# Order of a graph layer's first stage: a reload behind the last load, edge placing behind the statistics, first edge groups sooner

## The chip, the cores and the metric

The kernel runs on one core of a Trainium2 chip. The metric is the device time of one execution in microseconds (us). The engines are named as in the profile: PE (TensorE matmul), PEld (its weight loads), DVE (VectorE), ACT (ScalarE), POOL (GpSimd) and SP (SyncE, which here only issues DMAs). Each engine works through its own queue in order.

## The reference

One layer of a graph network on 10000 nodes with 512 features and 160000 edges, sorted by destination; everything is float32.

```python
xn = layernorm(x)
h  = xn @ W                                           # graph part
agg = segment_sum(h[src] * edge_weight[:, None], dst)
gnn = relu(agg + bias)
q, k, v = split(xn @ w_qkv.T)                         # 8 heads of 64
q = softmax(q, over a head's features) * 64 ** -0.5
k = softmax(k, over the nodes)
ctx = k.T @ v                                         # per head
mix = layernorm((q @ ctx) @ w_out.T) * gamma
x = x + gnn + mix
x = x + ffn(layernorm(x))                             # experts, weighted by a router on the mean row
```

## The kernel before

The nodes lie in 20 chunks: 19 of 128 partitions with 4 rows each (SUB = 4) and a last one of 68 partitions. The work has three stages, which the trace shows at 0 to 161 us, 161 to some 1850 us (the edges run through all of it) and from there to the end (the experts' products).

**Start.** `normal_rows` loads a chunk (L416, on SP's queue), takes its statistics on DVE (L166, L167), finishes them on POOL (L169, L171, L419, L420), normalises on ACT (L422) and stores the rows to a scratch tensor `xn_d` in DRAM (L424, ACT's queue). A pool of seven tiles (`a_io`) holds the chunks in flight. Meanwhile chunks 0 and 1 (`EARLY = 2`, the two that `KEPT` keeps in memory) do their keys and queries by plain matmuls (L209), exp and softmax (L885, `softmax_rows` with L192 to L194, `kacc` at L844), and the context sum over nodes `pc` (L911), which DVE copies or adds into `G` (L918, L914). Transposes on PE are L201, their evictions L203.

**Edge lists.** Four lists of 625 KB (`src_sb`, `w_sb`, `dst_sb`, `row_sb`; L446 to L451) are loaded on SP's queue after the statistics of `LISTS = 10` chunks. The generator `place_edges` (L454 to L518) then works out on DVE where in its window of nodes each edge falls; it is taken on by two steps after each further chunk (L428), and what is left of it at chunk 2 (L858).

**From chunk 2 on** keys and queries come from seven products instead of eight (`seven`, L246, with matmuls at L243); DVE makes the sums that they need: of the weights (`kq_sum`, L233 to L236, once) and of the rows (`xs_b`, L226 to L229, for each chunk). The rows come back from `xn_d` (`rows_of`, L834). Between products `work(us)` is called, which counts time in units of the code (`PRODUCT = 0.83` for a product of 128 by 128 by 512) and puts edge groups into PE's order as they come due: the number of tiles due is `done[1] / PACE` with `PACE = 0.9`. At chunk 2 the counter starts at

```python
done[1] = -16 * PACE
```

so nothing comes due for the first 16 tiles' worth of units.

**An edge group** has 8 tiles of 128 edges (4 from the 97th group on; 1250 tiles in all). For a tile, POOL gathers 128 rows of `xn_d` by index (`msg`, L583; 24 buffers in pool `edge_m`), DVE builds the selection matrix (`sel`, L589 and L591), PE multiplies (`pm`, L601), ACT copies the sum out (L604) and stores it to `part_d` (L605). Sums of nodes that cross windows are carried on by DMAs on POOL's queue (L673).

**Stage two** starts at about 1100 us. It mixes the queries with the context matrix and gathers the edge sums by row on POOL (`at`, L1017), while edge groups go on at `ROW_PACE = 0.96`; the last group is summed at about 1850 us. Then the experts' products follow, which don't touch the edges.

PE's order is the order of the code (`manual_schedule`, L708). The other engines' orders are set by the scheduler from readiness; `behind(inst, other)` (L157) makes it put one instruction after another, as an order only and without a semaphore. A buffer that lies over an older tile's memory also waits for the last user of that tile: `edge_m` is opened after `norm_ctx.close()` (L860), over the memory of the loads and of the placing's scratch tiles.

Of the kernel before, what the change touches and what calls it, by code (L numbers as in the profile page):

```python
# [12 lines left out]
ALU = mybir.AluOpType  # L13
# [7 lines left out]
SUB = 4  # L21
EPS = 1e-5
HEAD = 64
# [4 lines left out]
FAR = 1.0e5  # L28
EARLY = 2
ROWS_IN = 1.6  # L30
LISTS = 10
CHECKED = 5
KEPT = 2
PRODUCT = 0.83
PACE = 0.9
# [21 lines left out]
def gps_layer_kernel(  # L57
# [19 lines left out]
    nc = tc.nc  # L77
    N, D = x.shape
# [11 lines left out]
    chunks = []  # L90
# [8 lines left out]
    def tokens(t, c):  # L99
        b, r = chunks[c]  # L100
        return t[b : b + r * SUB, :].rearrange("(p s) d -> p s d", s=SUB)
# [38 lines left out]
    xn_d = dram.tile([N, D], F32, name="xn_d")  # L140
# [16 lines left out]
    def behind(inst, other):  # L157

        tc.add_manual_dep(inst.ins, other.ins.name, mybir.DependencyInfo(
            mybir.DependencyClass.NoSync, mybir.DependencyReason.SCHED_ONLY), reason="order of work")  # L160
# [27 lines left out]
    def softmax_rows(q, r, s):  # L188

        q3 = q[:r, s, :].rearrange("p (h e) -> p h e", e=HEAD)  # L190
        qs = small.tile([P, D // HEAD], F32, name="qs")
        nc.vector.tensor_reduce(qs[:r], q3, axis=AX.X, op=ALU.add)  # L192
        nc.vector.reciprocal(qs[:r], qs[:r])
        nc.vector.tensor_tensor(q3, q3, qs[:r, :, None].to_broadcast([r, D // HEAD, HEAD]), ALU.mult)  # L194

    def transposed(o, t, r, psum, tag, by_act=(1, 3)):

# [190 lines left out]
    with ExitStack() as ph:  # L388
# [16 lines left out]


        normal = []
        placing = []
        last_stats = [None]

        def normal_rows(n):

            for c in range(len(normal), min(len(normal) + n, NCH)):
                r = chunks[c][1]
                xt = (xp if c < KEPT else a_io).tile([P, SUB, D], F32, name="xn")
                nc.sync.dma_start(xt[:r], tokens(x, c))  # L416
                mv = small.tile([P, SUB, 2], F32, name="mv")
                last_stats[0] = row_stats(xt, r, mv, on_pool=True)
                nc.gpsimd.tensor_tensor(mv[:r, :, 0], mv[:r, :, 0], mv[:r, :, 1], ALU.mult)  # L419
                nc.gpsimd.tensor_scalar(mv[:r, :, 0], mv[:r, :, 0], -1.0, None, op0=ALU.mult)  # L420
                for i in range(SUB):
                    nc.scalar.activation(xt[:r, i, :], xt[:r, i, :], AF.Identity,  # L422
                                         bias=mv[:r, i, 0:1], scale=mv[:r, i, 1:2])
                nc.scalar.dma_start(tokens(xn_d, c), xt[:r])  # L424
                normal.append(xt)
                if len(normal) == LISTS:
                    placing.append(place_edges(*edges_listed()))
                for _ in range(2 if placing else 0):  # L428
                    next(placing[0], None)

        zero = tmp.tile([P, D], F32, name="zero")
        nc.vector.memset(zero, 0.0)
# [4 lines left out]
        place = ep.tile([P, NET], F32, name="place")  # L437
# [16 lines left out]
        def place_edges(dst_sb, row_sb):  # L454


            nc.vector.tensor_scalar(row_sb, row_sb, 2, None, op0=ALU.arith_shift_right)
            yield
            nc.vector.memset(bases[:, 0:1], 0.0)
            nc.vector.memset(bases[:, NW:], FAR)  # L460
            nc.vector.tensor_copy(bases[:, 1:PAIRED],
                                  row_sb[:, 2 : 2 * PAIRED].rearrange("p (w j) -> p w j", j=2)[:, :, 0])
            nc.vector.tensor_copy(bases[:, PAIRED:NW], row_sb[:, 2 * PAIRED :])
            yield
            gap = tmp.tile([P, NW], F32, name="gap")
            nc.vector.tensor_tensor(gap, bases[:, 1:], bases[:, :NW], ALU.subtract)
            yield
            nc.vector.tensor_copy(place, dst_sb)
            yield

            def by_window_of(t, per_window, o, op):

                nc.vector.tensor_tensor(
                    o[:, : 2 * PAIRED].rearrange("p (w j) -> p w j", j=2),
                    t[:, : 2 * PAIRED].rearrange("p (w j) -> p w j", j=2),
                    per_window[:, :PAIRED, None].to_broadcast([P, PAIRED, 2]), op)
                nc.vector.tensor_tensor(o[:, 2 * PAIRED :], t[:, 2 * PAIRED :], per_window[:, PAIRED:NW], op)

            nodes = tmp.tile([P, NW], F32, name="nodes")
            nc.vector.tensor_scalar(nodes, bases[:, :NW], float(SUB), None, op0=ALU.mult)  # L480
            yield
            by_window_of(place, nodes, place, ALU.subtract)
            yield

            nc.vector.memset(jump[:, 0:1], 1.0)
            nc.vector.tensor_scalar(jump[:, 1:], gap[:, : NW - 1], -1.0, float(WIN // SUB), op0=ALU.mult, op1=ALU.add)
            yield

            beyond = tmp.tile([P, NET], F32, name="beyond", tag="whole")
            good = tmp.tile([P, NET], F32, name="good", tag="row")  # L490
            nc.vector.tensor_scalar(nodes, gap, float(SUB), None, op0=ALU.mult)
            yield
            by_window_of(place, nodes, beyond, ALU.is_ge)
            yield
            nc.vector.tensor_scalar(nodes, nodes, float(SUB), None, op0=ALU.add)
            yield
            by_window_of(beyond, nodes, good, ALU.mult)
            yield
            nc.vector.scalar_tensor_tensor(place, place, float(SUB), good, op0=ALU.add, op1=ALU.subtract)
            yield  # L500
            nc.vector.scalar_tensor_tensor(good, place, float(SUB), beyond, op0=ALU.is_lt, op1=ALU.is_equal)
            yield
            nc.vector.scalar_tensor_tensor(good, place, float(WIN), good, op0=ALU.is_lt, op1=ALU.mult,
                                           accum_out=count[:, 0:1])
            yield
            nc.vector.tensor_scalar(good[:, :NW], gap, 0.0, None, op0=ALU.is_ge)
            yield
            nc.vector.scalar_tensor_tensor(good[:, : NW - 1], gap[:, : NW - 1], float(WIN // SUB), good[:, : NW - 1],
                                           op0=ALU.is_lt, op1=ALU.mult, accum_out=count[:, 1:2])
            yield  # L510
            nc.vector.tensor_scalar(good[:, CHAINED:NW], gap[:, CHAINED:], 0.0, None, op0=ALU.is_gt)
            nc.vector.tensor_reduce(count[:, 2:3], good[:, CHAINED:NW], axis=AX.X, op=ALU.add)
            yield

            for i, (n, w) in enumerate(AT_HAND):
                nc.vector.tensor_scalar(count[:, 3 + i : 4 + i], bases[:, w : w + 1],
                                        float((chunks[n][0] if n < NCH else N) // SUB), None, op0=ALU.is_ge)
            spans_hold()  # L518
# [164 lines left out]
        done = [0, 0.0]  # L683
# [146 lines left out]
        def rows_of(c):  # L830
            if c < KEPT:
                return normal[c]
            xn = xp.tile([P, SUB, D], F32, name="xn")
            nc.sync.dma_start(xn[: chunks[c][1]], tokens(xn_d, c))  # L834
            return xn

        def turned_rows(c, xn):
# [4 lines left out]
        def finish(o, ek, r, at):  # L842
            if o is ek:
                nc.vector.tensor_tensor(kacc[:r], kacc[:r], ek[:r, at, :], ALU.add)  # L844
            else:
                softmax_rows(o, r, at)

        wk = kvp.tile([P, KB, D], F32, name="wk")
        nc.sync.dma_start(wk, w_qkv_t[:, D : 2 * D].rearrange("(k p) d -> p k d", p=P))
# [4 lines left out]
        xn = rows_of(0)  # L854
        xnT = turned_rows(0, xn)
        for c, (_, r) in enumerate(chunks):
            if c == EARLY:
                for _ in placing[0]:  # L858
                    pass
                norm_ctx.close()  # L860
                pools["w"] = edge_ctx.enter_context(tc.tile_pool(name="edge_w", bufs=3))
                done[1] = -16 * PACE
                pools["m"] = edge_ctx.enter_context(tc.tile_pool(name="edge_m", bufs=24,
                                                                 reuse_waits="tile"))
            if c + 1 < EARLY:
# [5 lines left out]
            if c < EARLY:  # L871
                for o, w in ((ek, wk), (qt, wq)):
                    sums = []
                    for s in range(SUB):
# [8 lines left out]
                        for i, po in enumerate(sums):  # L883
                            at = s + 1 - len(sums) + i
# [17 lines left out]
                        finish(qt, ek, r, q)  # L902
            if c + 1 == EARLY:
                normal_rows(NCH)
                xn_next = rows_of(c + 1)
            if c + 1 < NCH:
                xnT = turned_rows(c + 1, xn_next)
# [26 lines left out]
            if c + 1 < NCH:  # L934
                xn = xn_next
# [127 lines left out]
        for c, (_, r) in enumerate(chunks):  # L1063
            ot, at = mixed.pop(0), ats.pop(0)
# [30 lines left out]
            if c == NCH - 1:  # L1095
# [3 lines left out]
                                           op0=ALU.mult, op1=ALU.mult)  # L1099
            if c < NCH - 1:  # L1100
                for s in range(SUB):
                    nc.vector.scalar_tensor_tensor(xsum[:r], ot[:r, s, :], mv[:r, s, 1:2], xsum[:r],
                                                   op0=ALU.mult, op1=ALU.add)
# [5 lines left out]
            if c == NCH - 2:  # L1109
# [7 lines left out]
                xn = rows_in(0)  # L1117
# [252 lines left out]
    with tc.manual_schedule(engines={mybir.EngineType.PE}):  # L1370
# [13 lines left out]
        xt = residual_rows(0)  # L1384
        for c in range(NCH):
            if c + 1 < NCH:
                xn = rows_in(c + 1)
# [6 lines left out]
            xt = nxt  # L1394

    any_more = nc.values_load(n_more[0:1, 0:1], min_val=0, max_val=1)
    with tc.If(any_more > 0):
# [9 lines left out]
        for c, (_, r) in enumerate(chunks):  # L1407
            n = SUB * r
            xn = rows_in(c)
# [3 lines left out]
            xt = fp.tile([P, SUB, D], F32, name="xt", bufs=2)  # L1413
            nc.sync.dma_start(xt[:r], z_d[c])
            hT = []
            for f in blocks:
                m, at = fsz[f], (f - NBASE) * P
# [55 lines left out]
```

## Time and profile before

| | us |
|---|---|
| median of 5 runs | 3304.11 |
| lowest and highest | 3296.22, 3306.65 |
| the profiled execution | 3305.32 |
| its span | 3303.6 |
| PE busy | 3194.3 (97%) |
| DVE busy | 1771.6 (54%) |
| POOL busy | 1314.9 (40%) |
| ACT busy | 833.9 (25%) |
| mean busy share of the DMA engines, first 100 us | 0.97 |
| clock granted to PE, mean | 0.987 |

The rows of a timeline give the start in us, the length in us, the engine, the line of the code, the operation, the output and inputs by the program's names, and the number of instructions taken together; in square brackets stands how long the engine had been idle and what ended the wait. A row of waits names the engine, the tile and line that waited, what it waited for, the total in us, the number of times and the longest. SPq and ACTq are DMA issues on the queues of SP and ACT. In fp32 each matmul of the code shows as two rows' worth of instructions (x4 is two matmuls of the code).

### The profile page before, as it was taken

Reading aid. Unit: us, or ns where it says so; the run is one execution under the profiler, and the core shown is the slowest. Engines: PE = TensorE matmul, PEld = TensorE weight load, DVE = VectorE, ACT = ScalarE, POOL = GpSimd, SP = SyncE. Lnnn points to the kernel's source line nnn. Section 1 sums busy time; section 2 is a strip of 40 time slices with the busy share of each in tenths; the row PEclk is TensorE's granted clock in tenths of the full one; section 3 lists DMA queues with packets and bytes.
Section 4 is the critical chain, followed back from the end, with each engine's and each line's share of the span. In section 5 each row is a group of like instructions: output and inputs, shape, how many; then the busy total and the mean of one; then the engine's idle time right before and its main releaser. Section 6 shows DMA issues by size and latency. Waiting matters only on the chain. (4 is left out here: it accounts for less than half of the span.)

```text
span 3303.6 us, 36142 instructions
## 1 busy us (share of the span) xinstructions
PE 3194.3 (97%) x12819; PEld 1899.0 (57%) x12819; DVE 1771.6 (54%) x3902; ACT 833.9 (25%) x1674; POOL 1314.9 (40%) x1421
## 2 busy tenths in 40 slices
PE   5899999999999999999998979999999999999998
PEld 3344444444443433333333358888888888888886
DVE  6655555555555356566665565445544554445533
ACT  5422222222222122222222142222232222222211
POOL 3377777777776777777777300000000000000000
PEclk8899999999999999999999989999999999999999
DMA  9678889888888999999999822121212212121111
GB/s 386 243 241 282 264 275 315 261 281 256 282 267 239 346 340 353 337 352 345 361 334 306 240 65 64 51 90 52 62 54 64 77 51 64 51 90 51 53 38 40
DMA packets 216735, 654.39 MB, mean 198 GB/s; under 512 B 34425, under 2 KB 74361, under 8 KB 188831
## 3 DMA queue, kind: packets, MB, share of 16 engines
q0 software_dynamic: 104096, 354.29, 33.3%
q1 hardware_dynamic: 69992, 175.33, 16.1%
q10 hardware_dynamic: 42452, 122.31, 9.5%
q8 instruction: 105, 1.72, 0.2%
q14 instruction: 90, 0.74, 0.1%
HBM read 491.21 MB, written 166.63 MB: 199 GB/s over the span
## 5 line engine op out<-in xcount | busy, mean ns | idle before, releaser
L583 POOL DMA_INDIRECT msg<-xn_d,src_sb x1250 | 1234.2, 987 | 431.6 <-issue 210.2
L601 PE MATMUL pm<-msg,sel 128*32 128x512 f32 x2504 | 363.9, 603 | 19.9 <-DMA msg<-xn_d,src_sb 17.5
L209 PE MATMUL pg<-wq,aT 128*128 128x512 f32 (+1 forms) x640 | 291.1, 602 | 0.0
L209 PE MATMUL po<-G,qT 128*128 128x512 f32 (+1 forms) x640 | 290.2, 600 | 0.0
L911 PE MATMUL pc<-xn,ek 128*128 128x512 f32 (+1 forms) x640 | 286.1, 597 | 0.0
L604 ACT COPY part<-pm 128x512 f32<-128x512 f32 x217 | 126.9, 585 | 626.9 <-PE pm L601 581.5
L601 PEld LDWEIGHTS pm<-msg,sel 128*32 128x32 f32 x2504 | 67.5, 109 | 283.1 <-issue 191.0
L209 PEld LDWEIGHTS pg<-wq,aT 128*128 128x128 f32 (+1 forms) x640 | 115.0, 187 | 175.6 <-issue 160.8
L243 PE MATMUL px<-xnT,w_sb 128*128 128x256 f32 (+1 forms) x800 | 204.9, 379 | 7.0 <-DVE u L1290 7.0
L209 PEld LDWEIGHTS po<-G,qT 128*128 128x128 f32 (+1 forms) x640 | 114.9, 187 | 162.9 <-issue 158.2
L166 DVE BATCH_NORM_STATS2 st<-ot 128x6 f32<-128x512 f32 (+1 forms) x160 | 110.5, 691 | 179.7 <-ACT ot L1052 179.0
L243 PE MATMUL p<-kq_sum,xs_b 128*128 128x512 f32 (+1 forms) x432 | 200.7, 600 | 0.0
L911 PEld LDWEIGHTS pc<-xn,ek 128*128 128x128 f32 (+1 forms) x640 | 118.3, 191 | 139.6 <-issue 131.5
L243 PE MATMUL px<-w_sb,hh 128*128 128x256 f32 (+1 forms) x800 | 185.8, 379 | 0.0
L243 PE MATMUL py<-xs,w_sum 128*128 128x256 f32 (+1 forms) x800 | 185.7, 375 | 0.0
L243 PE MATMUL py<-w_sum,hh 128*128 128x256 f32 (+1 forms) x800 | 179.2, 379 | 0.0
L243 PEld LDWEIGHTS px<-xnT,w_sb 128*128 128x128 f32 x800 | 150.7, 192 | 30.2 <-DVE u L1290 10.4
L243 PEld LDWEIGHTS px<-w_sb,hh 128*128 128x128 f32 (+1 forms) x800 | 150.3, 188 | 22.8
L243 PEld LDWEIGHTS py<-w_sum,hh 128*128 128x128 f32 (+1 forms) x800 | 150.0, 188 | 22.7
L243 PEld LDWEIGHTS py<-xs,w_sum 128*128 128x128 f32 x800 | 150.2, 191 | 20.1
L243 PEld LDWEIGHTS p<-kq_sum,xs_b 128*128 128x128 f32 (+1 forms) x432 | 78.0, 187 | 116.1 <-issue 89.8
L351 ACT ACTIVATE xn<-xn,st_all 128x128 f32<-128x128 f32 x288 | 114.8, 481 | 99.8 <-DMA xn<-x_d 94.1
(298 smaller groups left out, 4570.4 us busy)
## 6 DMA issues: line engine op xcount, KB each, us to landing
part_d<-part ACTq DMA_DIRECT2D x217, 256.0 KB
msg<-xn_d,src_sb POOLq DMA_INDIRECT x1250
xn<-in_x SPq DMA_DIRECT2D x19, 1024.0 KB
xn_d<-xn ACTq DMA_DIRECT2D x19, 1024.0 KB
qT_d<-qT ACTq DMA_DIRECT2D x19, 1024.0 KB
qT<-qT_d SPq DMA_DIRECT2D x19, 1024.0 KB
xt<-in_x SPq DMA_DIRECT2D x19, 1024.0 KB
x_d<-ot SPq DMA_DIRECT2D x19, 1024.0 KB
```

The source lines that it names most:

```text
L166: nc.vector.bn_stats(st[:r, s, :], t[:r, s, :])
L209: nc.tensor.matmul(po[:r, :], t[:, kb, s * r : (s + 1) * r], w[:, kb, :], start=kb == 0, stop=kb == KB - 1)
L243: nc.tensor.matmul(o, lhs[j], rhs[j], start=start and j == 0, stop=stop and j == n - 1, skip_group_check=True)
L351: nc.scalar.activation(xn[:, s, b * P : (b + 1) * P], xn[:, s, b * P : (b + 1) * P], AF.Identity, bias=st[:, b, s, 0:1], scale=st[:, b, s, ...
L583: nc.gpsimd.indirect_dma_start(out=m[k], out_offset=None, in_=xn_d, in_offset=bass.IndirectOffsetOnAxis(ap=src_sb[:, t0 + k : t0 + k + 1], ...
L601: nc.tensor.matmul(pm[h * WIN : (h + 1) * WIN, :], sel[:, k, :], m[k] if k < len(m) else m[0], start=j == 0, stop=j == batch - 1, skip_gro ...
L604: nc.scalar.copy(part, pm)
L911: nc.tensor.matmul(pc, ek[:r, s, cb * P : (cb + 1) * P], xn[:r, s, :], start=s == 0, stop=s == SUB - 1)
```

## The change

Four things change, all in the order of the start.

1. The reload of chunk 2's rows (`rows_of`, first use) is tied behind the last load of x.
2. `LISTS` goes from 10 to 18, and the placing is no longer taken on two steps at a time beside the statistics. Its first step is tied behind the statistics of the last chunk, and two later ones, with all that depends on them, behind the last softmax multiplication of chunk 1. (Only the steps that yield their instruction are tied: the shift of `row_sb`, and the update of `place` at L499.)
3. The counter of due tiles starts at `0 * PACE` at chunk 2 instead of `-16 * PACE`.
4. `softmax_rows` returns its last instruction, so that it can be tied to.

No instruction is added or removed on any engine.

```diff
-LISTS = 10
+LISTS = 18
...
-        nc.vector.tensor_tensor(q3, q3, qs[:r, :, None].to_broadcast([r, D // HEAD, HEAD]), ALU.mult)
+        return nc.vector.tensor_tensor(q3, q3, qs[:r, :, None].to_broadcast([r, D // HEAD, HEAD]), ALU.mult)
...
+        last_load = [None]
+        last_softmax = [None]
...
-                nc.sync.dma_start(xt[:r], tokens(x, c))
+                last_load[0] = nc.sync.dma_start(xt[:r], tokens(x, c))
...
                 if len(normal) == LISTS:
                     placing.append(place_edges(*edges_listed()))
-                for _ in range(2 if placing else 0):
-                    next(placing[0], None)
...
-            nc.vector.tensor_scalar(row_sb, row_sb, 2, None, op0=ALU.arith_shift_right)
-            yield
+            yield nc.vector.tensor_scalar(row_sb, row_sb, 2, None, op0=ALU.arith_shift_right)
...
-            nc.vector.scalar_tensor_tensor(place, place, float(SUB), good, op0=ALU.add, op1=ALU.subtract)
-            yield
+            yield nc.vector.scalar_tensor_tensor(place, place, float(SUB), good, op0=ALU.add, op1=ALU.subtract)
...
-            nc.sync.dma_start(xn[: chunks[c][1]], tokens(xn_d, c))
+            load = nc.sync.dma_start(xn[: chunks[c][1]], tokens(xn_d, c))
+            if c == KEPT:
+                behind(load, last_load[0])
...
-                softmax_rows(o, r, at)
+                last_softmax[0] = softmax_rows(o, r, at)
...
-                for _ in placing[0]:
-                    pass
+                for step in placing[0]:
+                    if step:
+                        behind(step, last_softmax[0])
...
-                done[1] = -16 * PACE
+                done[1] = 0 * PACE
...
                 normal_rows(NCH)
+                behind(next(placing[0]), last_stats[0])
                 xn_next = rows_of(c + 1)
```

In DVE's new order all placing steps but the cast of `dst_sb` (and the constants) stand after the statistics of the last chunk; those from L498 on (L499 of the kernel before) stand between the last softmax and the sums of chunk 2. In PE's new order the first edge group stands after the first `seven` of chunk 2 instead of the second.

## The prediction

> **What bounds the kernel now.** I began with the page. TensorE (PE) is busy for 97% of the span, in an order that is written out in the code, so the time is PE's work plus its waits. I then took the chain of waits per engine, for PE and for POOL, and after that the timeline around each large wait. PE's order can't bend round a late operand, hence each wait of its table is paid in full unless a later one shrinks by as much.
>
> ```profile
> PE 3194.3 (97%) x12819; PEld 1899.0 (57%) x12819; DVE 1771.6 (54%) x3902; ACT 833.9 (25%) x1674; POOL 1314.9 (40%) x1421
> L583 POOL DMA_INDIRECT msg<-xn_d,src_sb x1250 | 1234.2, 987 | 431.6 <-issue 210.2
> PE pm L601 <- DMA msg<-xn_d,src_sb: 17.5, 15, 3.6
> PE pt L201 <- DVE G L918: 13.8, 2, 13.4
> POOL msg L583 <- PE pm L601: 50.5, 132, 4.4
> ```
>
> PE waits 17.5 us in all for gathered messages. POOL's 40% is a mean over the span: the gathers run from 151 to 1840 us, and there they follow each other without a hole:
>
> ```profile
> 421.43 0.94 POOL L583 DMA_INDIRECT msg<-xn_d,src_sb  x1 [0.30 <-issue]
> 422.68 0.94 POOL L583 DMA_INDIRECT msg<-xn_d,src_sb  x1 [0.30 <-DMA msg<-xn_d,src_sb]
> ```
>
> Start to start is 1.25 us (0.95 of work, 0.30 between); the starts at 225.0 and 994 us are some 1.28 apart in the mean, because one in ten lasts longer. PE's pace for tiles is set by the code (0.9 of its units, with 0.83 a unit per product) and comes to the same rate. So up to about 1850 us two queues run side by side, and where gathers come from sets the end as much as PE does. The places that the change touches:
>
> ```profile
> 101.71 0.90 PE L201 MATMUL pt<-ident,qt 128*128 128x128 f32 x3 [13.36 <-DVE G L918]
> 115.33 0.33 SPq L834 DMA_DIRECT2D xn<-xn_d  x1
> 115.76 0.35 SPq L416 DMA_DIRECT2D xn<-in_x  x1
> 130.71 2.47 DVE L166 BATCH_NORM_STATS2 st<-xn 68x6 f32<-68x512 f32 x4 [14.40 <-DMA xn<-in_x]
> 151.37 1.26 POOL L583 DMA_INDIRECT msg<-xn_d,src_sb  x1 [13.24 <-DMA xn_d<-xn]
> 158.27 0.69 DVE L228 TENSOR_TENSOR xs_b<-xs_b,xnT 128x512 f32<-128x512 f32 x1
> 161.47 1.88 PE L243 MATMUL p<-kq_sum,xs_b 128*128 128x512 f32 x4
> 185.60 1.92 PE L601 MATMUL pm<-msg,sel 128*32 128x512 f32 x16
> 222.22 0.94 POOL L583 DMA_INDIRECT msg<-xn_d,src_sb  x1 [4.38 <-PE pm L601]
> 1045.01 0.96 POOL L583 DMA_INDIRECT msg<-xn_d,src_sb  x1 [8.01 <-DMA part_d<-part_d]
> 1045.34 5.09 PE L601 MATMUL pm<-msg,sel 128*32 128x512 f32 x15 [1.12 <-DMA msg<-xn_d,src_sb]
> 1844.13 4.47 PE L601 MATMUL pm<-msg,sel 128*32 128x512 f32 x6 [3.60 <-DMA msg<-xn_d,src_sb]
> ```
>
> The last load (68 rows) stands on SP's queue behind the reload of chunk 2, which waits for PE; DVE gets its rows at 130.71. Gathers can't start before the last rows are stored. At 222 POOL still waits for PE (it is 24 buffers ahead); at 1045 PE waits for POOL, and from 1793 to 1849 it does so six times.
>
> **The reload behind the last load.** SP's order then has L416 ahead of L834. The last load goes out near 98 us; DVE's 14.40 and ScalarE's wait behind it (14.26, to 136.15) go, and the last two stores of normalised rows leave near 120 and 124 instead of 139.10 and 142.51. On PE only 0.37 (exps late, 139.70) and 0.78 (144.62) of waiting hang on this.
>
> **The placing steps.** The sizes of L457 to L535 sum to about 19.4 us on DVE, spread today over 53 to 98 us between the statistics. All but the cast of dst (L468 today) leave that stretch. The first copy of G then comes when the loads allow: statistics of chunk 16 end at about 96.7, the copy at 97.2 instead of 100.98, so PE restarts some 4.1 earlier; the second wait there (0.40) goes, and the clock recovers earlier (below, 1.3). Chunk 1's keys start 5.3 earlier than 115.13, and with the waits above its transposes of chunk 2 start at 137.5 instead of 143.24: 5.7. Of the moved steps 14.3 us stand after the last statistics (112 to 130), where DVE is idle today: nothing. The rest is tied behind the last softmax, and there something is queued behind it: in the new order of DVE (lines of the changed kernel, durations of the same steps today) L498 1.43, L499 1.45, L501 1.52, L504 0.61, L506 1.14 and a G addition (0.60), 6.75 in all, stand ahead of the sums that chunk 2's first product reads (L228). These are ready at 158.96 today, 15.7 after 143.24; then at 137.5+15.7+6.75 = 159.95. PE would be there at 155.0 and waits 4.9. Chunk 2 starts 1.5 earlier than 161.47. Of 6.5 us gained, 5 are lost at once.
>
> **The gathers.** The second message buffer lies over a scratch tile of the placing, and the new order makes the second gather wait for the last placing step (L510). That ends 2.0 after L228 (L509 0.52, L229 0.60, L510 0.92), at 162.0. Today the second gather starts at 152.92, so the stream starts 9.1 later, although the stores are landed some 18 us earlier. What it gets back: POOL's waits for free buffers of 2.02, 0.64, 4.38 and 1.58 us, each less the 0.30 between any two gathers: 7.4, all gone when it is less far ahead. And gathers 2 to 10 take 13.0 us today against 8 x 1.25 = 10.0, beside DVE's long sums; I leave 1.2 of the 3.0, a gain of 1.8. Sum 9.1-7.4-1.8 = -0.1: at the message of 1045 us I take 0, with bounds of -4 (DVE leaves them alone) and +4 (the later buffer waits were not binding).
>
> **The edges, two groups earlier.** The first group stands after one set of seven products of chunk 2 instead of two, and all through PE's order up to the last forced groups 16 tiles lie earlier. A message is therefore wanted with 16 x 0.9 = 14.4 units less of other work before it; a product that the code calls 0.83 takes 0.86 (two rows of L243 x4 start 1.72 apart, two products each), 14.9 us. If gathers keep their times, PE has to wait: about 9 in the first groups (172 to 190), single ones of 1 to 2, and 5 to 8 at 1045. At that message it stands at today's time with 14.9 us more work left. This is the largest cost and it cancels the head start whatever that is.
>
> **The clock.** The granted clock in windows of 3.41 us: after the 4.26 us wait of PE that ended at 1098.49 it was 0.50 from 1096.23 for 6.83 us; also for 6.83 from 1792.55, after waits of 2.55 and 1.53 close together, the first of which filled 2.1 us of the window before; a wait of 1.74 at 1688 cost none. I take one new stretch of 6.83 at half clock: 3.4, with bounds 0 and 6.8. The Trainium skill ("TensorE: Matmul & The Clock Gate", Part 1: The HAM clock gate) says the clock halves after an idle window of some 3.4 us and comes back after a busy one. By it waits of 1 to 2 us cost no clock and the sum below would be 3.4 lower; the row at 1792.55 speaks against it, since no whole window was idle there.
>
> **What comes back.** After 1100 PE's waits for messages are landings. From 1793 to 1844 they are 2.55+1.53+1.17+1.77+1.20+3.60 = 11.8 us, and two stretches at half clock (6.83 and 3.41) cost some 4 of them: with PE 14.9 later in its work, gathers at their times are early enough, and 15.8 come back. The waits of 0.98, 0.64 and 1.74 before 1700 stay, as messages are wanted earlier until then, and I add 2.0 for them and their like (bounds 0 and 6). FFN (from 1930) keeps its work.
>
> Sum: 0 + 14.9 + 3.4 + 2.0 - 15.8 = +4.5. The profiled execution took 3305.3 (span 3303.6), so 3309.8; against the median of the five runs, 3304.1, it is 3308.6.
>
> **Rivals.** *Gathers keep up* (faster): with DVE's disturbance of POOL shifted, gathers run at 1.25 instead of 1.277 over the 670 that lead to 1045: 18 us, more than the 14.9. Then PE waits only in the first groups, and 4.5-14.9 = -10.4: 3293.7. For it: the rows at 421 and 422. Against: the slow ones are spread evenly, and the DVE work beside them doesn't change. It decides from a stream 7 us or more ahead of my sum at 1045. *The tail doesn't give back* (slower): its waits come from gathers queued behind carries and row loads on POOL, which then move with PE. If the 11.8 stay, 4.5+11.8 = +16.3: 3320.4. For it: the landings after 1100 are the longest, and POOL is busy there as well. Against: the last groups stand at the same place of PE's order, so gathers before them have the extra time. It decides once half of the 11.8 stays. *The change doesn't do what it says*: the lists are to come after eighteen chunks, yet in SP's order the first stands where it stood, after load 9, and the others only one load later; loads landing by 100 us thus gain nothing. This is in the sum already and has no time of its own.
>
> **The numbers.** My sum 0.43 (from -3 to +10 by the bounds together), gathers that keep up 0.26, a tail that gives nothing back 0.27, else 0.04. Differences under 0.2% (6.6 us) can't be told from none here; the five runs themselves spread over 10 us. Faster: 0.24, nearly the whole first rival. Slower: 0.27 and a third of my own case: 0.43. Within: 0.33. The range takes both rivals in: 3293 to 3322; my own case alone is 3301 to 3314.
>
> **What would show it.** Right: the first copy of G at about 97, the first product of chunk 2 near 160 with a wait of about 5 for L228 behind placing steps, the second gather near 162 released by DVE, PE's waits for messages above 15 us before 1100 and nearly none from 1790 to 1850. Wrong: POOL still waiting for buffers after 250 us (then gathers keep up), or waits of 1 to 4 at 1790 to 1850 as today; and any change after 1930 would lie outside of all this.

## The result and the profile after

The changed kernel took 3303.81 us (median of 26 runs, 3296.82 to 3311.73), the kernel before 3301.39 in 50 runs (3291.11 to 3308.76). The medians lie 2.4 us apart. The ratio is 1.0008, with a 95% interval from 1.0002 to 1.0014: 2.6 us slower, between 0.7 and 4.6. The interval just excludes a difference of nothing, but all of it lies inside the 0.2% (6.6 us) that I had called no change. The profiled execution lies 6.5 us above its median (3310.35, span 3308.6), so the 5.0 us between the two spans overstate the change; 2.2 of them arise after 1865 us, mostly in waits of the experts' products, which the change doesn't touch.

The waits by engine of the changed kernel (engine, tile and line that waited, releaser, total us, times, longest), of PE and then of POOL:

```profile
PE pm L599 <- DMA msg<-xn_d,src_sb: 21.8, 19, 2.8
PE pt L201 <- DVE G L920: 8.9, 1, 8.9
PE p L243 <- DVE xs_b L228: 4.3, 1, 4.3
```

```profile
POOL msg L581 <- PE pm L599: 42.5, 127, 2.5
POOL msg L581 <- DVE count L510: 25.7, 1, 25.7
```

PE's wait for the first copy of G is shorter by 4.5, that for the sums of chunk 2 is new, and POOL has a new wait of 25.7 us: the second gather, ready to go at 133.7, is held by the last placing step. The places in time, from the timeline of the changed kernel (lines are two to three off those of before):

```profile
95.99 0.90 PE L201 MATMUL pt<-ident,qt 128*128 128x128 f32 x3 [8.89 <-DVE G L920]
108.73 2.47 DVE L166 BATCH_NORM_STATS2 st<-xn 68x6 f32<-68x512 f32 x4 [0.36 <-DMA xn<-in_x]
132.44 1.26 POOL L581 DMA_INDIRECT msg<-xn_d,src_sb  x1 [13.41 <-DMA xn_d<-xn]
156.51 0.69 DVE L228 TENSOR_TENSOR xs_b<-xs_b,xnT 128x512 f32<-128x512 f32 x1
157.35 2.82 PE L243 MATMUL p<-kq_sum,xs_b 128*128 128x512 f32 x4 [4.29 <-DVE xs_b L228]
158.16 0.92 DVE L510 TENSOR_REDUCE count<-good 128x1 f32<-128x738 f32 x1
159.36 4.58 POOL L581 DMA_INDIRECT msg<-xn_d,src_sb  x1 [25.66 <-DVE count L510]
171.23 3.06 PE L599 MATMUL pm<-msg,sel 128*32 128x512 f32 x14
182.74 3.37 PE L599 MATMUL pm<-msg,sel 128*32 128x512 f32 x6 [0.22 <-DMA msg<-xn_d,src_sb]
225.87 0.95 POOL L581 DMA_INDIRECT msg<-xn_d,src_sb  x1 [0.30 <-issue]
1012.36 1.05 PE L599 MATMUL pm<-msg,sel 128*32 128x512 f32 x2 [2.12 <-DMA msg<-xn_d,src_sb]
1850.36 1.02 PE L599 MATMUL pm<-msg,sel 128*32 128x512 f32 x2 [2.48 <-DMA msg<-xn_d,src_sb]
1854.05 1.93 PE L599 MATMUL pm<-msg,sel 128*32 128x512 f32 x6 [2.67 <-DMA msg<-xn_d,src_sb]
```

The row at 182.74 needs care. Sixteen of these instructions take 1.92 when their messages are there (185.60 in the kernel before); here six take 3.37. PE waits between single matmuls for less than the table counts, and the row calls it busy. The first two groups run from 171.23 to 175.45 and from 179.08 to 186.04: 11.2 us where two times 1.85 would do. So PE loses 7.5 us in these two alone, while the list of waits shows under 1 us there. It is the messages: the 16th was issued at 181.5 and landed at 185.0, and the last two instructions of the second group start at 185.06 and 185.52. The row at 225.87 is the 51st gather; it stood at 225.04 in the kernel before. The same gather and the last one, from the timelines of the kernel before (L583), of the changed kernel, and of e6 and e5, which are told of below:

```profile
225.04 1.04 POOL L583 DMA_INDIRECT msg<-xn_d,src_sb  x1 [0.30 <-issue]
1846.44 0.95 POOL L583 DMA_INDIRECT msg<-xn_d,src_sb  x1 [0.30 <-issue]
1843.97 0.94 POOL L581 DMA_INDIRECT msg<-xn_d,src_sb  x1 [0.30 <-PE pm L599]
224.47 1.03 POOL L581 DMA_INDIRECT msg<-xn_d,src_sb  x1 [0.30 <-issue]
1839.84 0.95 POOL L581 DMA_INDIRECT msg<-xn_d,src_sb  x1 [0.30 <-issue]
1818.55 0.95 POOL L581 DMA_INDIRECT msg<-xn_d,src_sb  x1 [0.30 <-issue]
```

Landmarks, read from the timelines of these four profiles, none of which shows the idle time that some of the runs below have (starts in us; the last line but one is the start of the last matmul):

| | before | changed | e6 | e5 |
|---|---|---|---|---|
| first copy of G lets PE go on | 101.71 | 95.99 | 96.34 | 97.2 |
| second gather | 152.92 | 159.36 | 160.35 | 135.28 |
| chunk 2's first product | 161.47 | 157.35 | 158.34 | 154.87 |
| first edge group | 185.60 | 171.23 | 185.03 | 166.98 |
| gather 51 | 225.04 | 225.87 | 224.47 | 201.66 |
| gather 651 | 995.7 | 995.5 | 995.6 | 972.1 |
| last gather | 1846.4 | 1844.0 | 1839.8 | 1818.6 |
| last edge matmul | 1853.7 | 1854.9 | 1847.7 | 1828.6 |
| span | 3303.6 | 3308.6 | 3300.3 | 3278.1 |

From gather 51 to the last there are 1621, 1618, 1615 and 1617 us. Whatever the change does in front, that stretch is the same within 6 us, and the end goes where gather 51 goes. Only e5 moves gather 51 by more than those 6 us, and a difference as small as the 2.6 us can't be traced in this way.

### The profile page after: what moved, and what is told of

Read it like the earlier page. It is cut to its first block, busy times and chain, and to the rows that moved or that the text cites. A ratio compares the mean times of both kernels' runs of the same rounds, so it can differ in the third digit from the quotient of the medians.

```text
span 3308.6 us, 36153 instructions
## 1 busy us (share of the span) xinstructions
PE 3190.5 (96%) x12819; PEld 1897.2 (57%) x12819; DVE 1771.4 (54%) x3902; ACT 834.6 (25%) x1674; POOL 1312.5 (40%) x1421
## 5 line engine op out<-in xcount | busy, mean ns | idle before, releaser
L599 PE MATMUL pm<-msg,sel 128*32 128x512 f32 x2504 | 359.2, 604 | 22.4 <-DMA msg<-xn_d,src_sb 21.8
L243 PEld LDWEIGHTS py<-xs,w_sum 128*128 128x128 f32 x800 | 150.6, 192 | 20.2
L243 PE MATMUL p<-wk,xnT 128*128 128x512 f32 (+1 forms) x288 | 138.5, 603 | 1.6 <-ACT u L276 1.6
```

The costliest lines, as they stand in the source:

```text
L243: nc.tensor.matmul(o, lhs[j], rhs[j], start=start and j == 0, stop=stop and j == n - 1, skip_group_check=True)
L599: nc.tensor.matmul(pm[h * WIN : (h + 1) * WIN, :], sel[:, k, :], m[k] if k < len(m) else m[0], start=j == 0, stop=j == batch - 1, skip_gro ...
```

## The experiments

The theory (A): up to 1850 us the end is set by the stream of gathers. PE's head start is worth nothing, and earlier groups neither help nor hurt for themselves; the changed kernel has moved PE 4 us and the first group 14 us ahead, but not the stream, because the placing steps tied behind the softmax hold it. The rivals: the late start of the gathers costs by itself, the earlier groups cost by themselves, or the parts simply add.

Only e5 and e6 ran on a chip like that of the result, called undisturbed below. The others ran on two chips on which the engines stand idle again and again, from some 165 to 195 us on, until something outside of the core or something that the trace doesn't name (the kernel before took 3513 to 3534 us there). Their ratios are against the kernel before on the same chip. Of their traces the part before that idle time is read; where a later row is used, the text says what the idle time adds.

**e1_reload, e9_reload: the tied reload alone** (kernel before).

```diff
-            nc.sync.dma_start(xn[: chunks[c][1]], tokens(xn_d, c))
+            load = nc.sync.dma_start(xn[: chunks[c][1]], tokens(xn_d, c))
+            if c == KEPT:
+                behind(load, last_load[0])
```

> The kernel before with the reload of chunk 2 tied behind the last load, and nothing else. Theory A (up to 1850 us the end is set by when gathers come, and their lead is capped by 24 buffers): DVE's wait of 14.40 us for the last load goes, gathers start near 133 instead of 151, fill the buffers by about 163 and then wait for PE; PE itself gains about 1 us (waits of 0.37 and 0.78). Against before -2 to +0.5 us. Theory B (an earlier start of the gathers is kept to the end): the 18 us earlier start comes through, PE's waits from 1790 to 1850 (11.8 us) go: -8 to -12 us.

> The same kernel as e1_reload (kernel before with the reload tied), for the part after 180 us. Theory A, sharpened by e5 and e6: the whole stage to 1850 us shifts as one with the gathers, and their place is read where the 24 buffers first bind (start of gather 51: 225.0 in before, 225.9 changed, 201.7 in e5). Here the gathers start early but wait for the unmoved groups: gather 51 at 223 to 225, 0 to -2 against before. Rival (each part has its own worth and they add): the 18 us earlier start counts by itself, -6 or more.

Measured: ratio 1.0027 (1.0009 to 1.0044) and 1.0009 (0.9988 to 1.0029). The gathers do start 15 us earlier (136.16 in e9), but the stream then stops, as the timeline of e9 shows at gather 25:

```profile
189.71 0.95 POOL L584 DMA_INDIRECT msg<-xn_d,src_sb  x1 [21.38 <-PE pm L602]
```

With 24 buffers full, POOL waits 21.4 us for the first group (23.9 in e1). That group stands at 188.39 in e9 and at 185.60 in the kernel before, so idle time has some 3 us of the wait. The lead that an earlier start gives is used up while that group stays where it was. That the whole time doesn't fall is measured on these two chips alone, where it rules out the rival's -6 us; on an undisturbed chip this kernel wasn't run.

**e2_late_groups, e6_late_groups: the changed kernel with the counter back.**

```diff
-                done[1] = 0 * PACE
+                done[1] = -16 * PACE
```

> The changed kernel with the counter of due tiles back at -16 * PACE. Theory A: PE doesn't want messages sooner than before, so the waits of the first groups (about 9 us more than before in 157 to 200) vanish; the stream of gathers is at its place of before by 1045 us, and PE waits there and from 1790 to 1850 as before: within 2 us of before, 2 to 3 below the changed kernel. Rival (the late start of the gathers alone is what costs): the loss stays without the earlier groups, +2 to +6 against before.

> The same kernel as e2_late_groups (changed kernel, counter at -16 * PACE), again for the part after 180 us. Theory A: no waits in the first groups; the gathers reach 1045 us at the time of before, the end waits as before: 3299 to 3303, within 2 of before. Rival (the late gathers alone cost): 3303 to 3308, and waits for messages before 1000 us.

Measured: 1.0039 (1.0018 to 1.0061) on a chip with the idle time, and 3299.28 against 3299.95, ratio 1.0001 (0.9989 to 1.0013), on an undisturbed one. From the timeline of e6, chunk 2's first product and the second gather:

```profile
158.34 3.75 PE L243 MATMUL p<-kq_sum,xs_b 128*128 128x512 f32 x4 [4.28 <-DVE xs_b L228]
160.35 1.22 POOL L581 DMA_INDIRECT msg<-xn_d,src_sb  x1 [25.44 <-DVE count L510]
```

The second gather is as late as in the changed kernel, and still the time is that of before: with groups at 185 PE doesn't notice, and POOL's waits for buffers absorb most of the delay: those of 2.02, 0.64 and 4.38 us before gather 51 in the kernel before have shrunk to one of 0.82, and gather 51 stands at 224.5. The rival that the late gathers alone cost falls on this chip; on the other the kernel was 0.39% slower, which I can't read through the idle time.

**e4_no_softmax_tie, e5_no_softmax_tie: the changed kernel without the tie behind the softmax.**

```diff
-                for step in placing[0]:
-                    if step:
-                        behind(step, last_softmax[0])
+                for _ in placing[0]:
+                    pass
```

> The changed kernel without the tie of the placing steps behind the last softmax: on DVE they all stand in the idle time from 111 to 135 us, so the second gather isn't held (about 134 instead of 159) and L228 isn't late. Theory A: PE starts chunk 2 near 153 without its wait of 4.3, the first groups (near 165) find their messages, the waits of 157 to 200 go (about 9 and 1.3 of half clock), the end's waits stay as small as in the changed kernel: -10 to -16 against the changed kernel. Rival (POOL's own pace uses the lead up before 1045 us and PE waits there instead): first groups without waits, but 6 to 12 us of waits at about 1000 to 1050, and -4 to +1 against the changed kernel.

> The same kernel as e4_no_softmax_tie, for the part after 180 us, which stalls of all engines covered there. Its start is known from that run: chunk 2 at 154.7, the second gather at 136.3, first groups without waits. Theory A: the lead is kept and the small waits at the end of the changed kernel stay small: 3287 to 3294, -10 to -16 against the changed kernel (3304). Rival (POOL's pace uses the lead up): waits for messages of 6 to 12 us near 1000 to 1050, 3299 to 3305.

Measured: 0.9955 (0.9934 to 0.9976) in e4, and in e5 3279.56 us against 3299.95, ratio 0.9937 (0.9922 to 0.9953): 20.8 us faster than before (15.5 to 25.7), and by the ratio of the ratios (0.9937 / 1.0008, from two sets of runs) 23 us faster than the changed kernel. That is more than either account gave: theory A had the direction, and its -10 to -16 was too small. The timeline of e5 on POOL and PE, and its waits:

```profile
135.28 0.96 POOL L581 DMA_INDIRECT msg<-xn_d,src_sb  x1 [0.30 <-issue]
154.87 1.88 PE L243 MATMUL p<-kq_sum,xs_b 128*128 128x512 f32 x4
166.98 1.92 PE L599 MATMUL pm<-msg,sel 128*32 128x512 f32 x16
201.66 0.95 POOL L581 DMA_INDIRECT msg<-xn_d,src_sb  x1 [0.30 <-issue]
1825.19 4.50 PE L599 MATMUL pm<-msg,sel 128*32 128x512 f32 x10 [2.48 <-DMA msg<-xn_d,src_sb]
```

```profile
PE pm L599 <- DMA msg<-xn_d,src_sb: 10.9, 12, 2.7
```

All placing steps now lie on DVE between 113 and 133 us, most of it time in which DVE had nothing to do. The second gather starts 24.1 us earlier than in the changed kernel, chunk 2 doesn't wait for L228, and the first group finds its messages (sixteen instructions in 1.92). Gather 51 stands 24.2 us earlier, the last gather 25.4, the last edge matmul 26.3. The 24 us are kept for 1600 us. The same matmul of other work that came 20.2 us later than before in the changed kernel, near 1704, comes 1.8 earlier than before here. Removing the tie also takes away PE's wait for L228, but that is 4.3 us, too little for 21 to 23. This version is faster than both kernels.

**e3_early_groups, e10_early_groups, e13_early_groups: the counter at 0 alone** (kernel before).

```diff
-                done[1] = -16 * PACE
+                done[1] = 0 * PACE
```

> The kernel before with the counter at 0, and nothing else: groups 16 tiles earlier, gathers start at 151 as before. Theory A: gathers have their lead of about 20 us, so the first groups wait little, but PE stands at 1045 us with some 15 us more work left, and the waits from 1790 to 1850 (11.8 and 4 of half clock) come back: 0 to +4 against before. Rival (the earlier groups alone are good and only the late gathers spoil them): waits at 1045 don't grow and the 12 to 16 us of the end come back in full: -8 to -14.

> The same kernel as e3_early_groups (kernel before, counter at 0), for the part after 180 us. Theory A, sharpened: gathers start at 151 as before, but POOL's waits for buffers (7.4 us) go, gather 51 at about 217, -5 to -9 against before. My first account (PE waits at 1045 eat it): 0 to +4.

> The same kernel as e10_early_groups (kernel before, counter at 0), once more for the part after 180 us, where idle time without a releaser covered it in two runs. Their start is known: gather 1 at 150, first group at 172. Theory A: POOL's waits for buffers go, gather 51 at 216 to 219 instead of 225, -5 to -9 against before, and waits for messages at the end below 8 us. My first account (PE stands at 1045 with more work left): 0 to +4.

Measured, each on a chip with the idle time: 1.0009 (0.9988 to 1.0031), 1.0049 (1.0032 to 1.0066), 1.0030 (1.0007 to 1.0053). The sharpened theory wanted 5 to 9 us less, and none is faster. But it wanted gather 51 at 217; that gather stood at 222.9 in e3, 224.9 in e10 and 223.2 in e13, with POOL waiting for a PE that idle time had held, so the numbers don't test it. What earlier groups alone are worth on an undisturbed chip stays open.

**e11_reload_early, e14_reload_early: both, with the placing where it was** (kernel before, the diffs of e1 and e3).

> The kernel before with both the tied reload and the counter at 0; edge lists and placing steps stay where they were. Theory A: gathers from 133 on, first group at about 172, gather 51 at 206 to 210: -14 to -19 against before, more than the two parts alone together. Rival (the parts add): the sum of e9 and e10. Against e5 it tells what moving the placing behind the statistics is worth by itself: 4 to 6 us by PE's earlier start of chunk 2.

> The same kernel as e11_reload_early (kernel before, reload tied, counter at 0). Known: gathers from 134 to 137, first group at 172. Theory A: gather 51 at 205 to 209, -15 to -19 against before, while the reload alone gave nothing (it makes POOL wait 23.9 us for the first group). Rival (the parts add): no more than e13.

Measured: 0.9992 (0.9975 to 1.0010) and 1.0005 (0.9982 to 1.0028), on chips with the idle time; at least -14 us was expected and missed there. In one set of runs (e9, e10 and e11) the reload alone had 1.0009, the groups alone 1.0049 and both together 0.9992: they don't add, and with the groups moved the reload does count, which it didn't alone. The second pair (1.0030 in e13, 1.0005 in e14) points the same way within its noise. The wait of POOL for the first group, 21.4 us in e9, is nearly gone in e11's timeline, the first row; in e14, the second row, idle time of PE had put that group at 179.03 instead of 172.07, so its 11.9 us are mostly that:

```profile
173.39 0.94 POOL L584 DMA_INDIRECT msg<-xn_d,src_sb  x1 [1.77 <-PE pm L602]
180.35 0.95 POOL L584 DMA_INDIRECT msg<-xn_d,src_sb  x1 [11.91 <-PE pm L602]
```

Gather 51 stands at 210.6 in e11, at the edge of the forecast (217.5 in e14), and still nothing is won on that chip: there the end doesn't go where gather 51 goes.

The first group stands at 172.1 in e11 and at 166.8 in e4, the rest of the way being the head start that the moved placing gives to PE (chunk 2's first product at 159.96 and 154.70).

**e12_half_group_more: e5 with groups earlier still.**

```diff
-                done[1] = 0 * PACE
+                done[1] = 8 * PACE
```

> e5 (changed kernel without the tie behind the last softmax) with the counter at 8 * PACE: groups 8 tiles earlier still. Theory A: gathers can't start sooner (stores land at 133), so PE waits 1 to 5 us in the first groups; the waits at the end (6.8 us and a half clock stretch) come back in part: -6 to +1 against e5. Rival (the lead is used up): waits for messages at about 1000 of 5 us and more, +2 to +6 against e5.

Measured: 1.0052 (1.0031 to 1.0074), on a chip with the idle time, where e4 on another such chip had 0.9955. The idle time sets in here at 168: the second group takes from 168.2 to 178.7, though its messages (9 to 16) had landed between 147 and 162. So it isn't starved by the gathers, and the run says nothing on either account. One thing is read before that: chunk 2 starts at 154.0, the first group stands at 157.6 and takes its 1.9 us without waiting. Whether 8 tiles more gain or lose on an undisturbed chip stays open.

## Why the prediction was right, and where its steps were off

Forecast +4.5 with the range from 3293 to 3322, measured +2.6 and 3303.8. Sign and size hold, and so does the step that decides: the stream of gathers starts late and stays where it was. That the sum comes out so near is in part luck, since two of its terms, of 15 us each, cancel for a reason that the prediction didn't give. Of its signs of being right, the first copy of G, the late first product of chunk 2 and the second gather released by DVE came; message waits above 15 us before 1100 did not (5.2 in the list, some 12 with what the rows at 171 to 186 hide), nor did their absence at the end. Waits of 1 to 4 us between 1790 and 1850, which it had named as a sign of being wrong, are there. Step by step:

- **The start of PE.** The first copy of G was put at 97.2 and came at 95.28; chunk 2's transposes at 137.5, were at 134.66; the sums of chunk 2 at 159.95, were at 157.20; PE's wait for them 4.9, was 4.29. All came 2 to 3 us sooner, most of it because chunk 16's statistics ended at 95.3 and not at 96.7, and the half clock with them. The loss of 5 us to that wait was right, but it was 4.3 of 8.4 us and not 5 of 6.5 (without its wait PE would have started at 153.1), so chunk 2 starts 4.1 earlier and not 1.5. The steps behind the last statistics, put at 14.3 us, took 12 (111.66 to 123.65); nothing rested on it.
- **The second gather.** Put at 162.0, was at 159.36, and its releaser was the one named. But it took 4.58 us, so the third starts at 164.24, a microsecond later than in my sum. Net effect at gather 651: forecast -0.1, taken as 0, measured -0.2 (995.5 against 995.7). This term decided the result.
- **The work left over.** Forecast 14.9 us more to do at the same message, which with the 16 tiles already done (3.4 at 0.215 each) means that the same other work comes 18.3 later. Measured by the same matmul in both traces: 11.2 later near 230 us, 17.1 at 1094, 20.2 at 1704. Right in size, and nearly in place: the first groups were put at about 9 and lost 7.5, and the 5 to 8 at 1045 came at 1012, where the same work falls back from 14.9 to 22.4 later, with listed waits of 2.1 and 1.7. The kernel before then loses 4.8 itself at its row of 1045.34, which brings the distance to 17.6.
- **The clock.** One new stretch of 6.83 (3.4 us) was forecast. There were two of 3.41, at 158.3 after the 4.29 wait and at 1015.0 after 2.12 and 1.67 close together: 3.4 us in all. Neither had a wholly idle window before it: of the 3.41 us before 158.3 PE was idle for 2.5, of those before 1015.0 for 2.4. So the rule of the Trainium skill ("TensorE: Matmul & The Clock Gate", Part 1: The HAM clock gate) that I had weighed, a whole idle window, is too strict here.
- **What comes back: right sum, wrong account.** 15.8 were forecast. The same other work goes from 20.2 later to 2.8 later across the last groups, 17.4, of which 3.4 are tiles done ahead: 14.0. But the waits did not vanish, as I had written: five of 1.3 to 2.75 us, 10.6 in all, stand between 1810 and 1855, and the two half clock stretches of the end are there as before (3.41 from 1817, 6.83 from 1851). PE follows the last gathers one by one there in both kernels. The two terms, 14.9 lost and 15.8 won, are, as I read it, one: the end is where the stream ends, and the stream had not moved (last gather at 1844.0, before 1846.4). I could have had it from that alone.
- **The rivals.** *Gathers keep up* did not come in this kernel: gather 651 stands where it stood, and POOL's waits for buffers between 250 and 1009 us stay under 0.9. Its price of -10.4 was too small for a stream that is ahead: e5, a different kernel, has gather 651 23.6 us earlier and gains 21, so there the stream's start carries through nearly in full. *The tail doesn't give back*: its waits stayed and the time did not rise to 3320, so its condition did not mean what I had taken it to mean. The chance of slower was also mis-added: 0.27 and a third of 0.43 make 0.41, not 0.43.

## What to carry to other kernels

When two queues run in step for long, find the place from which the slower one runs on without long waits (here gather 51; the next ones come near 1000 us) and compare that place. In the four undisturbed profiles here the end followed it, and what PE gained in front without it was given back. An earlier start needs both ends, the producer let go (e5) and the consumer asking sooner (e9 shows the full buffers without the second, the changed kernel the late messages without the first). What the consumer's earlier asking is worth alone on an undisturbed chip is not shown. And a step tied "behind" something also holds back whoever waits for its memory: before tying it, look which tile will lie there next.

## What the runs showed of the hardware

- A gather's time on POOL is 0.95 us, but the one at 159.36 of the changed kernel took 4.58, while DVE made selection matrices from 159.00 to 163; before had one of 2.30 at 163.34, again beside them. The second gather of e6, at the same place of the order, took 1.22, so what makes it long isn't shown.
- On two of the chips the kernel before took 6 to 7% more (3513 to 3534 us against 3300 to 3301). ACT waits there for something that the trace puts outside the core, 42 times and 245.6 us in e9; none of the four undisturbed profiles has such a row. What it is isn't shown:

```profile
ACT part L605 <- remote: 245.6, 42, 18.7
```

The ranking of the kernels changed with it (e6 the same as before, its twin e2 0.39% slower), so in this case a gain of a few tenths of a per cent on one chip did not tell what the same program does on another.
